# State-space layers: one PSUM tile per recurrence, B rows spread on the array's row halves, the product written one recurrence ahead

## The chip, the cores and the metric

The kernel runs on one core of a Trainium2 chip, all of it in one launch. The metric is the device time of that launch in microseconds (us), the median of several runs. The engines are named as the profile names them: PE is TensorE (matmuls; PEld is its weight load), DVE is VectorE, ACT is ScalarE, POOL is GpSimd, and SP is SyncE, which issues the DMAs.

## The reference

The input x is 4 x 64 x 128 x 128 in float32 and goes through four layers: a Mamba block with 16 states, a window-transform layer, a convolution layer with a gate, and a block of two convolutions, a Mamba with 64 states and a feed-forward part. The change is in the two Mamba parts. Cut to what matters, with 65,536 tokens and 128 inner channels:

```python
xz = u @ in_proj_w.T;  xh, z = split(xz)
xc = silu(causal_conv(xh) + conv_b)            # 4 taps, per channel
dt, B, C = split(xc @ x_proj_w.T)              # B, C: one row per state
delta = softplus(dt @ dt_proj_w.T + dt_proj_b)
A = -exp(A_log)
def step(h, t):                                # per channel d and state n
    d, b, c, xt = t
    h = h * exp(d[:, None] * A) + (d * xt)[:, None] * b[None, :]
    return h, h @ c
y = scan(step) + xc * D
y = (y * silu(z)) @ out_proj_w.T
```

Layer 0 follows it with a projection, a layer norm over the channels, SiLU and the residual; layer 3 has a layer norm ahead of it and behind it.

## The kernel before, in words

Five stages run one after the other: layer 0, layer 1, the convolutions of layers 2 and 3, layer 3's Mamba, layer 3's feed-forward part. Both Mamba stages are one class, `_Mamba`, with its own constants.

**Tiling.** The tokens are cut into 64 chunks of TC = 1024. A *recurrence* is one `tensor_tensor_scan` on 128 partitions x 1024 tokens; its partitions are NQ = 4 states x DD = 32 channels. The 128 channels take ND = 4 recurrences, which make a *group* of 4 states. A chunk has 4 groups (16 recurrences) in layer 0, 16 groups (64 recurrences) in layer 3, so there are 5120 recurrences in all. The state is carried from chunk to chunk in `state` (L584).

**What one recurrence needs.** The decay da = exp(delta A) is made by ACT (L526) from `dl`, a row copy of delta out of DRAM. The input b x delta x x is made in one of two ways, which the strings "DADA" and "DADAADAADADAADAA" choose group by group:
- *Kind A* (3072 recurrences): ACT (28 small instructions a group, L401) and POOL (one block, L405) multiply transposed channels by B into `bxT`; PE transposes it into a PSUM tile with eight instructions a recurrence (L482), and the scan reads that tile.
- *Kind D* (2048): PE spreads the four B rows of the group over the partitions once for the group, straight from xc (four 128-row matmuls, L286, called from `produced`), into one PSUM tile. DVE multiplies that tile by `du` (a row copy of delta x, L559) into a second PSUM tile, which all four recurrences use, and the scan (L577) reads this one. So mul and scan take turns.

The scan writes into a place of `ring`, which has eight places in SBUF: recurrence i uses place i mod 8. POOL multiplies the place by `cb`, the spread C rows (L582). PE then sums over the states (L427): two halves of a group, four matmuls each, into the tile y. D times xc opens y (L424). After the last group DVE makes yg = y x silu(z) (L610), and the output projection follows (L619).

**PSUM.** Three tiles of two banks, bx0 to bx2, go round a list `idle`; y takes the other two banks. The recurrences' tiles and all of the pieces below are taken from the same three.

**Order.** `run()` writes the order by hand, one recurrence after the other, and `_Pin` makes each engine keep the order of writing. In the turn of recurrence i it loads `cb` (SP), lets pieces that wait for "next" go on, writes the exps up to five recurrences ahead, the due part of `bxT` (a credit, due two recurrences before the group), for kind D the product, PE's fills up to two recurrences ahead, the scan, POOL's product, and last the sums that are due, at most one half a turn. A group's sums are due two recurrences after its last (`owed`, i + 2); yg comes one turn after the last sums (`full`, i + 1).

**Pieces.** The rest of a chunk is written as generators whose parts are put at places counted in recurrences from the chunk's first (`slots`). `front()` makes z (wz), conv (the taps), v (delta and u = delta x), C (L334, with the copy L337), B (BT, L347 and L349) and duT (L356, L358) of the next chunk. `ahead()` in layer 3 has centre and norm ahead of it, `behind()` has project and rstd (layer 0) or project, centre2 and norm2 (layer 3). A piece takes a PSUM tile, PE fills it, and at the next turn ACT reads it and gives the tile back to the end of `idle`. SP issues every load and store in that order too: `cb` (L391), `dl` and `du` (L503), the stores of delta and u (L326, L328) and of the C rows (L341).

Of the kernel before, what the change touches and what calls it, by code (L numbers as in the profile page):

```python
# [17 lines left out]
P = 128  # L18
B, C, HH, WW = 4, 64, 128, 128
HW = HH * WW  # L20
TC = 1024
# [7 lines left out]
DA = 6  # L29
_PERM = np.arange(DI).reshape(DD, ND).T.reshape(-1)  # L30
# [137 lines left out]
class _Mamba:  # L168
# [19 lines left out]
    def __init__(self, ctx, tc, K, nst, w, kinds, bufs, slots={}):  # L188
# [8 lines left out]
        self.hold, self.parts, self.shared = False, {}, None  # L197
# [17 lines left out]
        nc.vector.memset(self.wz, 0.0)  # L215
        nc.sync.dma_start(self.wz[64:], w["in_wT"][:, DI:])
        self.wbc = cp.tile([P, 2 * nst], F32, name="wbc")
        nc.sync.dma_start(self.wbc, w["xp_bcT"])
        self.wC = cp.tile([P, max(nst, DD)], F32, name="wC")
        nc.vector.memset(self.wC, 0.0)  # L220
        nc.vector.tensor_copy(self.wC[:, :nst], self.wbc[:, nst:])
        self.spread = {}
        for g in (g for g, kind in enumerate(kinds) if kind == "D"):
            s = self.spread[g] = cp.tile([P, P], F32, name=f"spread{g}")
            nc.vector.tensor_copy(
                s.rearrange("p (q e) -> p q e", q=NQ),
                self.wbc[:, NQ * g : NQ * (g + 1)].unsqueeze(2).to_broadcast([P, NQ, DD]),
            )
# [36 lines left out]
    def shift(self, b):  # L265

        for k, ws in (("conv_b", self.taps), ("z_b", [self.wz])):
            pm, col = self.pm(), self.cp.tile([P, 1], F32, name=f"{k}_shift")
            for i, wt in enumerate(ws):
                self.nc.tensor.matmul(pm[:, :1], wt, b, start=i == 0, stop=i == len(ws) - 1)  # L270
            self.nc.vector.tensor_scalar(col, pm[:, :1], getattr(self, k), None, ALU.add)
            setattr(self, k, col)
# [6 lines left out]
    def slot(self, c, name):  # L279
        return "at", c["no"] * self.ng * ND + self.slots[name]  # L280

# [13 lines left out]
    def front(self, c, S, read, before_silu=None):  # L295

        nc, K, nst = self.nc, self.K, self.nst
        xc, sz = c["xc"], c["sz"] = [self.t(k, self.bufs[k]) for k in ("xc", "sz")]
        yield self.slot(c, "z")
        pm = self.take()  # L300
        self.mm(pm, (self.wz, S[:, 2:]))
        yield "next", 0
        self.hold = True
        nc.scalar.activation(sz, pm, AF.Silu, bias=self.z_b)  # L304
        self.give(pm)
        yield self.slot(c, "conv")
        pm = self.take()
        self.mm(pm, (self.taps[0], S[:, :TC]), (self.taps[1], S[:, 2:]))
        read()
        yield "next", 0  # L310
        if before_silu:
            before_silu()
        nc.scalar.activation(xc, pm, AF.Silu, bias=self.conv_b)
        self.give(pm)
        yield self.slot(c, "v")
        pm = self.take()
        self.mm(pm, (self.wdt, xc))
        yield "next", 0
        pos, du = self.tmp("pos"), self.tmp("u")
        nc.scalar.activation(pos, pm, AF.Softplus, bias=self.dt_b)  # L320
        self.give(pm)
        nc.scalar.preload_act_table_set(SET6)
        self.hold = False
        d2 = c["d2"] = self.dram.tile([2, DI, TC], F32, name="d2", tag="d2")
        c["dl"], c["du"] = {}, {}
        nc.sync.dma_start(d2[0], pos)  # L326
        nc.gpsimd.tensor_mul(du, pos, xc)
        nc.sync.dma_start(d2[1], du)  # L328

        yield self.slot(c, "C")  # L330
        r = self.wC.shape[1]
        pm = self.take(0)
        for h in range(NH):
            nc.tensor.matmul(pm[r * h : r * (h + 1)], self.wC, xc[:, _COLS[h]], start=True, stop=True)  # L334
        yield "next", 0
        cr = self.t("cr", 1, 512)
        nc.scalar.copy(cr[: 2 * r], pm[: 2 * r])  # L337
        self.give(pm)
        c["C"] = self.dram.tile([nst, TC], F32, name="c2", tag="c2")
        for h in range(NH):  # L340
            nc.sync.dma_start(c["C"][:, _COLS[h]], cr[r * h : r * h + nst])  # L341

        yield self.slot(c, "B")
        BT = c["BT"] = self.wp.tile([P, NB, nst], F32, name="BT", tag="BT")
        pm = self.take(0)
        for k in range(NB):
            nc.tensor.matmul(pm[:, nst * k : nst * (k + 1)], xc[:, P * k : P * (k + 1)], self.wbc[:, :nst], start=True, stop=True)  # L347
        yield "next", 0
        nc.scalar.copy(BT.rearrange("p k n -> p (k n)"), pm[:, : nst * NB])  # L349
        self.give(pm)  # L350

        yield self.slot(c, "duT")
        duT = c["duT"] = self.wp.tile([P, NB, DI], F32, name="duT", tag="duT")
        pm = self.take()
        for k in range(NB):
            nc.tensor.transpose(pm[:, P * k : P * (k + 1)], du[:, P * k : P * (k + 1)], K.eye)  # L356
        yield "next", 0
        nc.scalar.copy(duT.rearrange("p k d -> p (k d)"), pm)  # L358
        self.give(pm)


    def take(self, half=None):

        if half is None:
            t = self.idle.pop(0)
            self.parts[id(t)] = [t, 1]
            return t
        if self.shared is None:
            t = self.idle.pop(0)
# [8 lines left out]
    def give(self, ap):  # L378
# [6 lines left out]
        self.idle.append(t)  # L385
# [49 lines left out]
    def run(self, chunks, ahead, behind, lead):  # L435
# [24 lines left out]
        das, tiles = {}, {}  # L460
# [15 lines left out]
        def produced(i):  # L476

            v, j = its[i]
            if v["kind"] == "A":
                bx = tiles[i] = self.idle.pop(0)  # L480
                for k in range(NB):
                    nc.tensor.transpose(  # L482
                        bx[:, P * k : P * (k + 1)], v["bxT"][:, k, :, :, j].rearrange("p q e -> p (q e)"), self.K.eye
                    )
            elif not j:
                bx = v["B"] = self.idle.pop(0)
                self.mm(bx, (self.spread[v["g"]], v["c"]["xc"]))
# [18 lines left out]
        for _ in ahead(chunks[0]):  # L506
            pass
        replicated(-1)
        pin()
        for i, (u, j) in enumerate(its):  # L510
# [9 lines left out]
            for f in [f for f in feeds if f[1][0] == "next"]:  # L520
                step(f)

            while not self.hold and nexp < min(n, i + 5) and its[nexp][1] in its[nexp][0]["c"].get("dl", ()):
# [7 lines left out]
            for v in groups[max(nmul - 1, 0) : nmul + 2]:  # L531
                if "duT" in v["c"] and v["at"] > i:
                    left += 0 if "bxT" in v else NQ * (NB - 1)
                    slope = max(slope, left / (upto[max(v["at"] - 2, i + 1)] - upto[i]))
            credit += slope * (upto[i + 1] - upto[i])
            while credit >= 0.5:
# [10 lines left out]
            credit = min(credit, 0.5)  # L547

# [4 lines left out]
            if u["kind"] == "D":  # L553
                if not j:
                    while nbx <= i:
                        produced(nbx)
                        nbx += 1
                    u["y"] = self.idle.pop(0)
                nc.vector.tensor_mul(u["y"], u["c"]["du"][j], u["B"])  # L559
                tiles[i] = u["y"]  # L560
                if j == ND - 1:
                    self.idle.append(u["B"])
            due = [f for f in feeds if f[1][0] == "at" and f[1][1] <= i] if u["kind"] == "D" and j < ND - 1 else []
            while nbx <= min(n - 1, i + 2):
                v, k = its[nbx]
                if v["kind"] == "D" and k:
                    nbx += 1
                    continue
                if nbx > i and (not self.idle or (due and len(self.idle) < 2) or (v["kind"] == "A" and (("bxT" not in v) or (todo and v is groups[nmul - 1])))):
                    break  # L570
                produced(nbx)
                nbx += 1
# [7 lines left out]
            if u["kind"] == "A" or j == ND - 1:  # L580
                self.idle.append(tiles[i])
# [4 lines left out]
            for f in due:  # L586
                step(f)
            if i == u["at"] and u["g"] == 0:
                owed.append((u["last"], u, None))
            if i == u["last"]:  # L590
                owed += [(i + 2, u, h) for h in range(NH)]
            while owed and not full and (owed[0][0] <= i or i + 1 == n):
                _, v, h = owed.pop(0)
                self._sums(v, h)
                if v["g"] == self.ng - 1 and h == NH - 1:
                    full = i + 1, v["c"]
                if i + 1 < n:
                    break
            replicated(i)
# [26 lines left out]
def layer0(ctx, tc, K, w, x, x1):  # L626
    nc = tc.nc
    slots = {"z": -16, "conv": -15, "v": -14, "C": -8, "B": -7, "duT": -6, "project": 24, "rstd": 25}
    m = _Mamba(ctx, tc, K, 16, w, "DADA", {"xc": 2, "sz": 3, "tmp": 4}, slots)
# [53 lines left out]
    def behind(c, yg):  # L683
        c["res"] = m.t("res", 2, 512)
        for h, src in enumerate(_halves(x[c["at"][0]], c["at"][1])):
            nc.sync.dma_start(c["res"][64 * h : 64 * (h + 1)], src)
# [14 lines left out]
        m.give(pm)  # L701
        nc.gpsimd.tensor_mul(o, pc, o)

# [572 lines left out]
def layer3_mamba(ctx, tc, K, w, t3, x3, s3, n3):  # L1276

    nc = tc.nc
    slots = {"centre": -44, "norm": -43, "z": -32, "conv": -31, "v": -30, "C": -24, "B": -23, "duT": -22}
    slots |= {"project": 72, "centre2": 73, "norm2": 74}  # L1280
    m = _Mamba(ctx, tc, K, 64, w, "DADAADAADADAADAA", {"xc": 2, "sz": 2, "tmp": 4}, slots)
# [23 lines left out]
    def ahead(c):  # L1305
# [23 lines left out]
        m.give(pm)  # L1329
        nc.gpsimd.tensor_mul(S[:, 2:], xs, sq)  # L1330
# [5 lines left out]
    def behind(c, yg):  # L1336
        b, t0 = c["at"]
        tr, xr = m.t("tr", 1, 512), m.t("xr", 1, 512)
# [14 lines left out]
        xs, o = m.t("ncr", 1, 512), m.t("o", 1, 512)  # L1353
# [8 lines left out]
        m.give(pm)  # L1362
        nc.gpsimd.tensor_mul(o, xs, o)
# [287 lines left out]
```

## Time and profile before

| | |
|---|---|
| device time, median of three runs | 18174.38 us (18161.99 to 18198.42) |
| profiled execution: its own time, its span | 18180.54 us, 18178.8 us |
| granted TensorE clock, mean | 0.892 |
| busy share PE, PEld, DVE, ACT, POOL | 78%, 39%, 86%, 79%, 76% |
| layer 0: yg products (L610), first 426.2 to tenth 880.6 us | 50.45 us a chunk |
| layer 3: yg products, 5827.0 to 17220.7 us for 64 | 180.85 us a chunk |

The profile records one execution. The span is the time from its first to its last instruction. Each group of instructions is a line of the kernel with an engine, an operation, the tile written and the tiles read; a wait is the idle time of an engine ahead of an instruction, with the instruction that released it. The share of busy time is an average over five stages with different limits, so the stages are looked at separately, in windows of the trace. The clock is what the throttle granted PE, as a share of full speed.

### The profile page before, as it was taken

How to read it: one execution, taken by the hardware profiler on the slowest of the kernel's cores; microseconds unless marked ns; L12 is line 12 of the kernel's file. 1: busy time of each engine (PE TensorE's matmuls, PEld its weight loads, DVE VectorE, ACT ScalarE, POOL GpSimd, SP SyncE). 2: the span in 40 equal slices, each digit the busy share in tenths (PEclk: the TensorE clock that was granted, in tenths of full speed). 3: DMA queues.
4: the chain of work that ended last, by engine and by line, in shares of the span. 5: the costliest groups of instructions: out<-in, count | busy, mean ns of one | idle time of the engine just before them, and what ended most of it. 6: DMA issues, size and time to landing. Idle time of an engine off the chain costs nothing. (4 is left out here: it accounts for less than half of the span.)

```text
span 18178.8 us, 232945 instructions
## 1 busy us (share of the span) xinstructions
PE 14201.9 (78%) x77626; PEld 7167.2 (39%) x77626; DVE 15626.1 (86%) x8611; ACT 14325.0 (79%) x29853; POOL 13839.1 (76%) x7966
## 2 busy tenths in 40 slices
PE   7788788798997777777777777777777777777799
PEld 3333333387344333333333333333333333333333
DVE  8999999522116999999999999999999999999987
ACT  8888889212336999999999999999999999999733
POOL 7888889300005999999999999999999999999800
PEclk9999999789998888888888888898888888888899
DMA  6666666211212333232333333323333333333222
GB/s 162 168 167 170 168 168 172 66 44 59 70 40 81 90 82 92 81 91 82 90 83 90 84 88 84 88 84 89 84 88 84 88 84 89 84 89 83 74 55 55
DMA packets 669499, 1722.52 MB, mean 95 GB/s; under 512 B 196784, under 2 KB 231936, under 8 KB 660864
## 3 DMA queue, kind: packets, MB, share of 16 engines
q1 hardware_dynamic: 668288, 1707.62, 34.6%
q8 instruction: 608, 9.96, 0.2%
q14 instruction: 603, 4.94, 0.1%
HBM read 1434.27 MB, written 272.63 MB: 94 GB/s over the span
## 5 line engine op out<-in xcount | busy, mean ns | idle before, releaser
L582 POOL TENSOR_TENSOR ring<-ring,cb 128x1024 f32<-128x1024 f32 x5120 | 12048.3, 2375 | 1119.3 <-DVE ring L577 1064.3
L577 DVE TENSOR_TENSOR_SCAN ring<-da,state,bx 128x1024 f32<-128x1024 f32 x4848 | 11070.8, 2332 | 343.4 <-PE bx L482 83.6
L401 ACT ACTIVATE bxT<-duT,BT 128x128 f32<-128x128 f32 x21504 | 6770.9, 388 | 110.2 <-PE bx L482 110.2
L526 ACT ACTIVATE da<-dl,A 128x1024 f32<-128x1024 f32 x5120 | 5809.7, 1139 | 501.1 <-DVE ring L577 483.6
L482 PE MATMUL bx<-cst,bxT 128*128 128x128 f32 x24576 | 4101.7, 320 | 1947.7 <-DVE bx L559 861.1
L482 PEld LDWEIGHTS bx<-cst,bxT 128*128 128x128 f32 x24576 | 3490.8, 212 | 3626.3 <-DVE ring L577 1474.3
L427 PE MATMUL y<-ring,cst 128*32 128x512 f32 x20480 | 3548.2, 671 | 336.7 <-POOL ring L582 336.6
L559 DVE TENSOR_TENSOR bx<-du,bx 128x1024 f32<-128x1024 f32 x2048 | 2503.3, 1222 | 131.1 <-ACT da L526 47.8
L427 PEld LDWEIGHTS y<-ring,cst 128*32 128x32 f32 x20480 | 517.5, 113 | 1885.3 <-POOL ring L582 833.2
L1143 PE MATMUL cv<-img,cw 64*64 64x512 f32 x9216 | 1010.1, 595 | 73.1 <-DMA img<-d_x 45.6
L286 PE MATMUL bx<-xc,spread 128*128 128x512 f32 x2048 | 1019.5, 620 | 0.2
L1301 POOL MEMSET X<- 64x1 f32 x4 | 0.4, 102 | 1123.4 <-DMA cw<-in_l_conv_wT 1123.4
L405 POOL TENSOR_TENSOR bxT<-duT,BT 128x512 f32<-128x512 f32 x768 | 803.8, 1047 | 6.4 <-ACT duT L358 6.4
L347 PE MATMUL bx<-wbc,xc 128*128 128x16 f32 (+1 forms) x2048 | 391.3, 360 | 449.1 <-ACT cr L337 333.0
L1068 POOL TENSOR_TENSOR xs<-xs,cl 128x1024 f32<-128x1024 f32 x32 | 75.9, 2371 | 861.8 <-DVE cl L1067 861.8
L286 PE MATMUL bx<-S,cw 128*128 128x512 f32 x1024 | 536.0, 671 | 248.2 <-ACT sz L304 248.2
L1143 PEld LDWEIGHTS cv<-img,cw 64*64 64x64 f32 x9216 | 490.9, 134 | 590.5 <-issue 479.4
L1438 POOL MEMSET h<- 128x18 f32 x64 | 8.3, 132 | 875.1 <-PE pd L1526 443.0
L1452 ACT ACTIVATE h<-ph,ff_fc_b 128x384 f32<-128x384 f32 (+1 forms) x384 | 200.7, 577 | 593.2 <-PE ph L1447 575.4
L286 PEld LDWEIGHTS bx<-xc,spread 128*128 128x128 f32 x2048 | 349.9, 191 | 760.4 <-issue 476.4
L1526 PE MATMUL pd<-h,diag 64*64 64x512 f32 x4608 | 631.6, 602 | 0.7 <-issue 0.7
L577 DVE TENSOR_TENSOR_SCAN ring<-da,bx 128x1024 f32<-128x1024 f32 x272 | 604.7, 2272 | 31.0 <-PE bx L482 10.2
(311 smaller groups left out, 10931.8 us busy)
## 6 DMA issues: line engine op xcount, KB each, us to landing
cb<-c SPq DMA_DIRECT2D x5120, 128.0 KB, 2.9
dl<-d SPq DMA_DIRECT2D x2048, 128.0 KB, 3.4
du<-d SPq DMA_DIRECT2D x2048, 128.0 KB, 3.3
d<-pos SPq DMA_DIRECT2D x128, 512.0 KB, 3.0
d<-u SPq DMA_DIRECT2D x128, 512.0 KB, 3.0
X<-d_t SPq DMA_DIRECT2D x124, 256.0 KB, 4.1
S<-in_x SPq DMA_DIRECT2D x120, 256.5 KB, 3.9
res<-in_x SPq DMA_DIRECT2D x128, 128.0 KB, 3.2
```

Source lines behind the costliest of these rows:

```text
L286: self.nc.tensor.matmul(out[: l.shape[1], k : k + 512], l, r[:, k : k + 512], start=i == 0, stop=i == len(pairs) - 1)
L347: nc.tensor.matmul(pm[:, nst * k : nst * (k + 1)], xc[:, P * k : P * (k + 1)], self.wbc[:, :nst], start=True, stop=True)
L401: nc.scalar.activation(t[:, k, q].rearrange("p e j -> p (e j)"), c["duT"][:, k, :], AF.Copy, scale=c["BT"][:, k, n : n + 1])
L405: nc.gpsimd.tensor_mul(t[:, k].rearrange("p q e j -> p q (e j)"), c["duT"][:, k].unsqueeze(1).to_broadcast(shape), c["BT"][:, k, NQ * g : ...
L427: nc.tensor.matmul(c["y"][DD * j : DD * (j + 1), _COLS[h]], K.sel, hc[:, _COLS[h]], start=False, stop=u["g"] == self.ng - 1,)
L482: nc.tensor.transpose(bx[:, P * k : P * (k + 1)], v["bxT"][:, k, :, :, j].rearrange("p q e -> p (q e)"), self.K.eye)
L526: nc.scalar.activation(das[nexp], v["c"]["dl"][k], AF.Exp, scale=self.A[:, k, v["g"] : v["g"] + 1])
L559: nc.vector.tensor_mul(u["y"], u["c"]["du"][j], u["B"])
L577: nc.vector.tensor_tensor_scan(hs, das.pop(i), tiles[i], 0.0 if u["c"].get("reset") else st, ALU.mult, ALU.add)
L582: nc.gpsimd.tensor_mul(hc, hs, u["cb"])
L1143: nc.tensor.matmul(p[i][half[h]], W[half[i], k, :], src[half[i], at : at + 4, dx : dx + WW], start=k == 0, stop=k == 8,)
L1526: nc.tensor.matmul(pd[i][half[h]], diag[half[i], k, :], h0[half[i], r : r + 4, dx : dx + WW], start=k == 0, stop=k == 8,)
```

## The change

It is confined to `_Mamba` and the two stages that use it.

- Each D recurrence gets a PSUM tile of its own, like an A recurrence. B and C rows are projected together, once a chunk, by `wboth`, and copied by ACT into an SBUF tile `bc`, on both halves of the partitions. From there two matmuls per recurrence spread the four rows of the group: half h of the tokens uses the array's rows 64h and up (`rows`, the new `spread`, which is a selection out of the identity).
- DVE multiplies in place (`times`), and the product of recurrence i+1 is written ahead of the scan of i, wherever its tile was filled in an earlier turn.
- z is projected on the two row halves too (`wz` on both).
- PE's fills for the turn come in two parts, one ahead of the scan and one after it and after the sums. Tiles that pieces give back go to a list `late` and become idle with the scan's tile.
- Pieces get other places: conv ahead of z; B before duT before C in layer 3; the C rows at -11 instead of -24; the pieces behind one to three recurrences later. ACT's reads of pieces come after the exps, in layer 3 after up to three `bxT` parts. The product u and the norm products on POOL come one turn later, and the residual's load of layer 0 later still, with one buffer. In layer 3, xc has one buffer instead of two, and four small tiles come from the shared `tmp`.
- Sums are due three recurrences after a group's last instead of two, yg two turns after the last sums instead of one, and `bxT` is due four recurrences before its group instead of two.

The diff, cut to its core:

```diff
+BEHIND = 2
+LATER = 3
+EXPS = 5
+DUE = 4
...
+        for h in range(NH):
+            for k in range(2):
+                a = DD * k if self.small else 64 * (h ^ k)
+                nc.vector.tensor_copy(self.wboth[:, h, a : a + nst], self.wbc[:, nst * k : nst * (k + 1)])
...
+    def rows(self, bc, h, k):
+        a = 64 * h + DD * k if self.small else 64 * (h ^ k)
+        return bc[a : a + self.nst, :512] if self.small else bc[a : a + self.nst, _COLS[h]]
...
+        def both(pm):
+            for h in range(NH):
+                out = pm[64 * h : 64 * (h + 1), :512] if self.small else pm[:, _COLS[h]]
+                nc.tensor.matmul(out, self.wboth[:, h], xc[:, _COLS[h]], start=True, stop=True)
...
+    def free(self):
+        if not self.idle:
+            self.idle, self.late = self.late, []
+        return self.idle.pop()
...
-        self.idle.append(t)
+        self.late.append(t)
...
+            else:
+                for h in range(NH):
+                    r = slice(64 * h, 64 * h + self.nst)
+                    nc.tensor.matmul(bx[:, _COLS[h]], self.spread[v["g"]][r], self.rows(v["c"]["B"], h, 0), start=True, stop=True)
+
+        def times(k):
+            v, j = its[k]
+            if v["kind"] == "D" and k not in done:
+                done.add(k)
+                nc.vector.tensor_mul(tiles[k], v["c"]["du"][j], tiles[k])
+
+        def fill(i, upto):
+            nonlocal nbx
+            while nbx < min(n, upto) and self.idle:
+                v = its[nbx][0]
+                if nbx > i and v["kind"] == "A" and ("bxT" not in v or (todo and v is groups[nmul - 1])):
+                    break
+                if nbx > i and v["kind"] == "D" and "B" not in v["c"]:
+                    break
+                produced(nbx, i)
+                nbx += 1
...
-            if u["kind"] == "D":
-                if not j:
-                    while nbx <= i:
-                        produced(nbx)
-                        nbx += 1
-                    u["y"] = self.idle.pop(0)
-                nc.vector.tensor_mul(u["y"], u["c"]["du"][j], u["B"])
-                tiles[i] = u["y"]
...
+            fill(i, max(i + 1, min(nbx + 1, i + 3)))
+            times(i)
+            if i + 1 < n and filled.get(i + 1, i) < i:
+                times(i + 1)
             slot = i % (2 * ND)
...
-            if u["kind"] == "A" or j == ND - 1:
-                self.idle.append(tiles[i])
+            fresh = len(self.idle)
+            self.idle += [tiles[i]] + self.late
+            self.late = []
...
-                owed += [(i + 2, u, h) for h in range(NH)]
+                owed += [(i + LATER, u, h) for h in range(NH)]
...
-                    full = i + 1, v["c"]
+                    full = i + BEHIND, v["c"]
...
+            free, self.idle = self.idle[fresh:], self.idle[:fresh]
+            fill(i, i + 3)
+            self.idle += free
+            for f in [f for f in feeds if f[1][0] == "at" and f[1][1] <= i]:
+                step(f)
...
-    slots = {"z": -16, "conv": -15, "v": -14, "C": -8, "B": -7, "duT": -6, "project": 24, "rstd": 25}
+    slots = {"conv": -16, "z": -14, "v": -13, "C": -8, "B": -6, "duT": -5, "project": 24, "rstd": 26}
...
-    slots = {"centre": -44, "norm": -43, "z": -32, "conv": -31, "v": -30, "C": -24, "B": -23, "duT": -22}
-    slots |= {"project": 72, "centre2": 73, "norm2": 74}
+    slots = {"centre": -43, "norm": -41, "conv": -32, "z": -30, "v": -28, "B": -23, "duT": -21, "C": -11}
+    slots |= {"project": 73, "centre2": 75, "norm2": 77}
```

## The prediction

> **What bounds the kernel now.** I read the page's groups first. VectorE (DVE) is busy 86% of the span, and most of that is one scan per recurrence (L577) and, for 2048 of the 5120 recurrences, one product ahead of it (L559). The columns are busy us, mean ns, idle us before, and what ended the idle time.
>
> ```profile
> L577 DVE TENSOR_TENSOR_SCAN ring<-da,state,bx 128x1024 f32<-128x1024 f32 x4848 | 11070.8, 2332 | 343.4 <-PE bx L482 83.6
> L559 DVE TENSOR_TENSOR bx<-du,bx 128x1024 f32<-128x1024 f32 x2048 | 2503.3, 1222 | 131.1 <-ACT da L526 47.8
> ```
>
> Then I read two windows, layer 0 in steady state and the layer-3 state-space stage (columns: window, length, busy us of PE, PEld, DVE, ACT, POOL, granted clock, DMA share, GB/s). VectorE is the fullest engine in both, at 97% in the second; only there does work saved on it shorten the span.
>
> ```profile
> 400.00:3000.00 2600.00, 2084.04 (x10398) 970.22 (x10399) 2442.87 (x1289) 2323.60 (x4433) 2311.16 (x1289) 0.93 0.65 168
> 6200.00:17200.00 11000.00, 8197.02 (x41282) 4126.62 (x41283) 10679.69 (x5412) 10071.52 (x22002) 10267.47 (x5841) 0.88 0.31 86
> ```
>
> The periods come from the 64 yg products. Layer 3: (17220.7-5827.0)/63 = 180.85 us a chunk. Layer 0: ten from 426.2 to 880.6, nine intervals, 50.45 us. In them POOL is busy 168.8 and 44.8 us, ACT 165.6 and 45.1, PE 134.8 and 40.4.
>
> Then VectorE's timeline, across one D group and into A recurrences (start, length, instruction):
>
> ```profile
> 10034.36 1.21 DVE L559 TENSOR_TENSOR bx<-du,bx 128x1024 f32<-128x1024 f32 x1
> 10035.71 2.35 DVE L577 TENSOR_TENSOR_SCAN ring<-da,state,bx 128x1024 f32<-128x1024 f32 x1
> 10038.09 1.23 DVE L559 TENSOR_TENSOR bx<-du,bx 128x1024 f32<-128x1024 f32 x1
> ...
> 10168.82 1.20 DVE L610 TENSOR_TENSOR yg<-y,sz 128x1024 f32<-128x1024 f32 x1
> 10169.94 1.22 DVE L559 TENSOR_TENSOR bx<-du,bx 128x1024 f32<-128x1024 f32 x1
> ```
>
> In the D group mul to scan is 10035.71-10034.36 = 1.35 us (others 1.36), scan to the next mul 2.38: each is held by the one before, since the product waits for the shared tile and the scan for the product. A mul that nothing holds follows L610 after 1.12. A scans in a row start 2.24 apart although each lasts 2.35. So a D group takes 10046.93-10034.36+2.24 = 14.81 us, and VectorE's floor is 40x2.24+6x14.81+1.12 = 179.58 us in layer 3 (1.27 of 180.85 is stall) and 8x2.24+2x14.81+1.12 = 48.66 in layer 0 (1.79 of 50.45).
>
> Last, the waits. In layer 3 little holds VectorE (82.7 us in 11,000), so its stall is small; in layer 0 it waits for TensorE's sums, and ScalarE waits for TensorE's pieces:
>
> ```profile
> DVE ring L577 <- PE bx L482: 82.7, 62, 2.4
> ```
> ```profile
> ACT xc L313 <- PE bx L286: 132.2, 52, 4.7
> ACT BT L349 <- PE bx L286: 96.8, 51, 3.3
> DVE yg L610 <- PE y L427: 92.4, 29, 4.8
> ```
>
> [...] eight transposes take 1.23 or 1.98 us and eight sums matmuls 1.07 or 1.94. [...] four 64-row matmuls of 384 columns (L1447) take 0.92 us, four 128-row ones of 512 (L286) 1.98.
>
> **The change, part by part.**
>
> 1. *Product one recurrence ahead.* All but 192 of the 2048 muls now stand ahead of the previous scan, in a tile of their own. A pair costs 1.12+2.24 = 3.36 us, a group 13.44: 1.37 less. The 192, where a piece holds a tile, remain next to their scan (1.36, 0.24 more each), one per chunk in layer 3, two in layer 0. Layer 3: 6x1.37-0.24 = 7.98, floor 171.60. Layer 0: 2x1.37-2x0.24 = 2.26, floor 46.40. Over 64 chunks of each: 655 us. I take this in full.
>
> 2. *B rows spread per recurrence.* A D group had one spread of four matmuls (1.98 us); it now has four pairs of 64-row matmuls. Its price between 0.5 (side by side, full clock) and 2.0 (one after the other, half); I take 1.1, from L1447. PE grows by 4x1.1-2.0 = 2.4 per group, some 11 with smaller edits: 146 of 171.6, not the bound. A spread starts at a scan's end and its mul comes 3.36 us later, so 1.1+0.2 is covered by the mul and scan between; at 2.0 it still is. Without that cover (the 192) it costs up to 1.5. One copy of B and C on ACT (1.0 for 0.56 us) is 0.45 a chunk in layer 3, hidden by ACT's 15 us of room.
>
> 3. *Sums three recurrences late, not two.* The four-matmul halves (L427) stand on PE behind a fill that itself waits for a scan. The ring has eight places, so a group's first scan waits for the sums of the group two before. With two, the fill's scan lay three recurrences back; now it lies two back. So the chain scan end, fill, sums, next scan is set beside one scan of 2.24 us:
>
> ```profile
> 10051.57 1.23 PE L482 MATMUL bx<-cst,bxT 128*128 128x128 f32 x8 [0.63 <-DVE ring L577]
> 10052.73 1.07 PE L427 MATMUL y<-ring,cst 128*32 128x512 f32 x8
> ...
> 10018.84 1.98 PE L482 MATMUL bx<-cst,bxT 128*128 128x128 f32 x8 [0.26 <-DVE ring L577]
> 10020.75 1.94 PE L427 MATMUL y<-ring,cst 128*32 128x512 f32 x8
> ```
>
> Full clock: 0.16 (scan end to fill)+1.16+1.06-2.24 = 0.14. Half: 0.16+1.91+1.93-2.24 = 1.76. A head with a mul just ahead of its scan has cover, so I count those without: nine a chunk, eight plain and one behind the BT piece (L347) too. The clock is 1.00 or 0.50 in short windows, so 0.88 means 24% half; PE gets fuller, so I take 15% (bounds 5 to 53). A plain head costs 0.14+0.15x1.62 = 0.38, eight 3.1. The ninth waits behind BT's 16 matmuls (3.0 us); between 0.9 and 3.4, I take 2.0. In layer 0 one head stands behind BT and rstd: 1.3 to 3.25, I take 1.8. Lower bound for all: nothing, if PE runs ahead.
>
> 4. *Pieces moved.* Two old stalls go: 1.27 behind the duT piece in layer 3, and 1.79 in layer 0, where yg waited for sums behind conv (5.40 us of PE at 1028.20). They are not counted again, since I start from floors. What is late next is the conv piece, now ahead of z: 0.7 in layer 3, 0.4 in layer 0 (nothing to 1.5). The C row loads get about 11 recurrences, 27 us, against 2.9 of landing. The product u (POOL) and its store, res, and the norm products come a recurrence later, and their readers at least seven; SP issues as many DMAs, POOL and SP have the same queue behind them otherwise. Zero, covered by those recurrences; if this cover failed, some 3 us a chunk.
>
> **Sum.** Layer 3: 171.60+3.1+2.0+0.7 = 177.4, 3.45 less, 221 us. Layer 0: 46.40+1.8+0.4 = 48.6, 1.85 less, 118 us. Together 339 off the profiled execution's 18180.5 (span 18178.8): 17,842. The median of the runs, 18174.4, is 6 lower, so I say 17,840. Own range 17,600 to 18,060: the stalls of 3 and 4 halved give some 17,600; those of the slow clock at 30% with upper ends for BT and conv some 18,060.
>
> **Rivals.**
> - *The full gain stays* (0.19). Sums are ahead of need and only the conv piece and a BT rest show: layer 3 172.5, layer 0 47: 64x(8.35+3.45) = 755 off, about 17,430. For it: PE has 25 us of room a chunk. Against: VectorE already runs within 1.27 of its floor, so any new PE delay shows at once.
> - *Slower: sums behind a waiting fill at the group heads* (0.18). Nine heads break even at 3.45+5.8 = 9.3 us a chunk, 1.03 each, which is a half-clock share near 53%. If the new order leaves PE waiting on scans more often and the share is 70%, layer 3 is near 184 to 186 and layer 0 50: about 18,490. For it: stretches like 10016 to 10022 are at half clock just where PE waits for each scan. Against: 0.88 on average.
> - *ScalarE bounds layer 0.* Its 45.1 and the 265 us in 51.5 chunks that it waits for PE (5.15) make 50.2, so layer 0 gains nothing: 17,960, inside my own range. POOL's 168.8 lies under 171.6 and 177 and does not decide.
> - *Gains and stalls cancel* (0.06): 18,140 to 18,216.
> - *It doesn't do what it says*: excluded, since the order of instructions has 1856 muls ahead.
>
> **How the numbers follow.** Likeliest case 0.57, with ScalarE's; full gain 0.19; cancel 0.06; slower 0.18. A measurement here tells about 0.2%, 36 us, from no change. So faster 0.76, same 0.06, slower 0.18. The range, 17,430 to 18,330, takes in the full gain's centre and the lower part of the slower case. It leaves out about 0.08 below and 0.11 above.
>
> **What would show it.** Right: muls start 1.12 before a scan and 2.24 after one, a D group takes 13.44 us, yg comes every 177 and 48.6 us, and VectorE's new waits are for the sums at group heads, some 3 to 5 us a chunk. Wrong: D pairs at 3.7 (step 1), muls waiting for spreads (2), no wait for sums or one over 1 us a head (3), yg still waiting for sums (4), or a clock far from 0.9.

## The result and the profile after

The changed kernel is slower: 18803.43 us, median of four runs (18789.44 to 18810.32), against 18168.19 before (now of four runs); the ratio is 1.0346, with a 95% interval of 1.0328 to 1.0363. The forecast was faster, 17,840, with a range that ended at 18,330.

The profiled execution took 18807.81 us, 627 more than that of before. By the first and last scan of each stage in the two traces, 207 us of this lie in layer 0 and 416 in layer 3's Mamba; the other stages are within 6. From the scan starts of the 60 middle chunks the periods are 53.8 us in layer 0 (50.4 before) and 187.6 in layer 3 (181.0).

The same lines of the page's groups as before (busy us, mean ns, idle us ahead, what ended it). The scan's idle time has gone from 343 to 1100 us, and TensorE's sums end it:

```profile
L628 DVE TENSOR_TENSOR_SCAN ring<-da,state,bx 128x1024 f32<-128x1024 f32 x4848 | 11136.1, 2332 | 1100.1 <-PE y L467 1000.0
L529 PE MATMUL bx<-bc,spread 64*128 64x512 f32 (+1 forms) x8192 | 2650.3, 730 | 1597.9 <-DVE ring L628 1561.6
L535 DVE TENSOR_TENSOR bx<-du,bx 128x1024 f32<-128x1024 f32 x2048 | 2477.7, 1210 | 309.5 <-PE bx L529 145.7
```

The second line holds the other half of the story: the short spreads (L529) have 1598 us of idle TensorE ahead of them. The two windows of before, taken again (length, busy us of PE, PEld, DVE, ACT, POOL, granted clock, DMA share, GB/s). VectorE is busy less and TensorE more; the clock fell from 0.93 to 0.83 in layer 0 and from 0.88 to 0.86 in layer 3:

```profile
400.00:3000.00 2600.00, 2252.34 (x10923) 1002.03 (x10922) 2260.20 (x1210) 2181.71 (x4148) 2164.08 (x1209) 0.83 0.61 158
6200.00:17200.00 11000.00, 8543.82 (x44106) 4000.79 (x44105) 10133.95 (x5221) 9751.79 (x21234) 9934.02 (x5639) 0.86 0.31 83
```

VectorE's timeline over the end of a D group and its head (the first scan of the next group, of kind A), start and length:

```profile
9998.21 2.33 DVE L628 TENSOR_TENSOR_SCAN ring<-da,state,bx 128x1024 f32<-128x1024 f32 x1
10000.46 1.20 DVE L535 TENSOR_TENSOR bx<-du,bx 128x1024 f32<-128x1024 f32 x1
10001.58 2.33 DVE L628 TENSOR_TENSOR_SCAN ring<-da,state,bx 128x1024 f32<-128x1024 f32 x1
...
10004.94 4.57 DVE L628 TENSOR_TENSOR_SCAN ring<-da,state,bx 128x1024 f32<-128x1024 f32 x2
10011.46 2.35 DVE L628 TENSOR_TENSOR_SCAN ring<-da,state,bx 128x1024 f32<-128x1024 f32 x1 [1.95 <-PE y L467]
```

Scan to mul is 2.25 us and mul to scan 1.12, as step 1 of the prediction had it. Then the head at 10011.46 waits 1.95 us. TensorE over the same time:

```profile
9997.23 1.13 PE L529 MATMUL bx<-bc,spread 64*128 64x512 f32 x4 [1.24 <-DVE ring L628]
10000.59 1.13 PE L529 MATMUL bx<-bc,spread 64*128 64x512 f32 x4 [2.24 <-DVE ring L628]
10003.97 1.98 PE L673 MATMUL bx<-tx,cst 128*64 128x512 f32 x4 [2.24 <-DVE ring L628]
10005.72 1.93 PE L674 MATMUL bx<-yg,woT 128*64 128x512 f32 x4
10007.58 1.61 PE L467 MATMUL y<-ring,cst 128*32 128x512 f32 x8
10009.12 1.23 PE L523 MATMUL bx<-cst,bxT 128*128 128x128 f32 x8
10010.27 1.07 PE L467 MATMUL y<-ring,cst 128*32 128x512 f32 x8
```

A spread takes 1.13 us and TensorE then sits idle for 2.24 us until the next scan gives a tile back. After two such stretches the project piece runs at half rate (L673, 1.98 us for four matmuls, at a granted clock of 0.50), and behind it stand one half of the sums, a fill and the other half, for which the scan at 10011.46 waits. 30 us later the drop from 1.00 to 0.50 can be seen: the same spread takes 1.13, then 2.08, and the centre piece behind it 3.78 where it took 1.98 before:

```profile
10030.90 1.13 PE L529 MATMUL bx<-bc,spread 64*128 64x512 f32 x4 [1.24 <-DVE ring L628]
10034.27 2.08 PE L529 MATMUL bx<-bc,spread 64*128 64x512 f32 x4 [2.24 <-DVE ring L628]
10037.64 3.78 PE L301 MATMUL bx<-X,cst 128*128 128x512 f32 x4 [1.29 <-DVE ring L628]
```

### The profile page after: what moved, and what is told of

It is laid out like the page before. It is cut to its first block, busy times and chain, and to the rows that moved or that the text cites. A ratio compares the mean times of both kernels' runs of the same rounds, so it can differ in the third digit from the quotient of the medians.

```text
span 18806.0 us, 244842 instructions
## 1 busy us (share of the span) xinstructions
PE 15270.9 (81%) x83770; PEld 7295.5 (39%) x83770; DVE 15397.7 (82%) x8623; ACT 14362.4 (76%) x29853; POOL 13859.8 (74%) x7966
## 4 chain that ended last, share of the span: by engine, by line
PE 25%; DVE 21%; ACT 10%; issue 8%; DMA 2%; POOL 1%; SPq 1%; DVEq 0%; POOLq 0%; ACTq 0%
DVE ring L628 15%; PE bx L523 6%; DVE bx L535 6%; PE y L467 6%; ACT da L584 4%; ACT bxT L441 4%; PE bx L301 4%; PE pd L1586 3%; PE bx L357 1%; PE bx L352 1%; DMA cb<-c 1%; POOL ring L634 1%; PE ph L1507 1%; PE bx L673 1%; PE po L1551 1%
## 5 line engine op out<-in xcount | busy, mean ns | idle before, releaser
L584 ACT ACTIVATE da<-dl,A 128x1024 f32<-128x1024 f32 x5120 | 5734.2, 1138 | 353.4 <-DVE ring L628 333.7
L523 PE MATMUL bx<-cst,bxT 128*128 128x128 f32 x24576 | 3774.3, 303 | 719.6 <-DVE ring L628 656.2
L523 PEld LDWEIGHTS bx<-cst,bxT 128*128 128x128 f32 x24576 | 3288.5, 210 | 2664.3 <-DVE ring L628 1696.7
L529 PE MATMUL bx<-bc,spread 64*128 64x512 f32 (+1 forms) x8192 | 2650.3, 730 | 1597.9 <-DVE ring L628 1561.6
L467 PE MATMUL y<-ring,cst 128*32 128x512 f32 x20480 | 3117.6, 683 | 7.8 <-POOL ring L634 7.8
L535 DVE TENSOR_TENSOR bx<-du,bx 128x1024 f32<-128x1024 f32 x2048 | 2477.7, 1210 | 309.5 <-PE bx L529 145.7
L529 PEld LDWEIGHTS bx<-bc,spread 64*128 64x128 f32 (+1 forms) x8192 | 696.7, 206 | 3189.0 <-DVE ring L628 2850.0
L467 PEld LDWEIGHTS y<-ring,cst 128*32 128x32 f32 x20480 | 429.7, 115 | 1630.6 <-issue 1228.7
L301 PE MATMUL bx<-S,cw 128*128 128x512 f32 x1024 | 702.7, 851 | 298.2 <-DVE ring L628 285.2
L1532 DVE SCALAR_TENSOR_TENSOR g<-h,dww,g 128x2048 f32<-128x2048 f32 x256 | 601.9, 2351 | 11.0
```

The lines of the kernel that those rows point to most:

```text
L301: self.nc.tensor.matmul(out[: l.shape[1], k : k + 512], l, r[:, k : k + 512], start=i == 0, stop=i == len(pairs) - 1)
L467: nc.tensor.matmul(c["y"][DD * j : DD * (j + 1), _COLS[h]], K.sel, hc[:, _COLS[h]], start=False, stop=u["g"] == self.ng - 1,)
L523: nc.tensor.transpose(bx[:, P * m : P * (m + 1)], v["bxT"][:, m, :, :, j].rearrange("p q e -> p (q e)"), self.K.eye)
L529: nc.tensor.matmul(bx[:, _COLS[h]], self.spread[v["g"]][r], self.rows(v["c"]["B"], h, 0), start=True, stop=True)
L535: nc.vector.tensor_mul(tiles[k], v["c"]["du"][j], tiles[k])
L584: nc.scalar.activation(das[nexp], v["c"]["dl"][k], AF.Exp, scale=self.A[:, k, v["g"] : v["g"] + 1])
```

## The experiments

Four theories were set against each other: **A**, the sums come too late for the ring, because they are due one recurrence later and stand behind fills and pieces; **B**, TensorE is too slow altogether; **C**, the sums hold the fills while they wait for POOL; **D**, the clock is the cause. A time without an interval is that of one execution; executions of one kernel differ by 0.2% here (18160 to 18198 us before the change), and the differences between such times that a conclusion rests on are larger.

**later2**: the sums due as before the change.

```diff
-LATER = 3
+LATER = 2
```

> The changed kernel with the sums of a group due two recurrences after its last, as before the change, and nothing else altered. Theory A (the loss is the ring: a group's first scan waits for the sums of the group two before, and these now come one recurrence later, behind a fill or a piece that itself waits for a scan): each half gets one scan of 2.24 us more, so the waits of scans for L467 fall from some 13 us a layer-3 chunk to under 4 and from 4.8 to under 2.6 in layer 0; the periods go from 187.6 to about 177 and from 53.8 to about 51, and the time to 17,850 to 18,100 us. Theory B (TensorE is too slow in all: half clock and more matmuls, the waiting scan only shows it): the waits move to the muls or to other heads, and the time stays above 18,600 us. Theory C (the sums now wait for POOL's products and hold the fills behind them): waits of scans for L523 instead, time near 18,400.

Measured 18685.32, clock 0.882. That is 118 us under the changed kernel, outside what theory A gave and inside theory B's. The scans' wait for L467 is gone, but most of it has come back elsewhere. The waits in the layer-3 window (us, times, longest):

```profile
DVE bx L535 <- PE bx L529: 601.9, 270, 5.6
PEld y L467 <- POOL ring L634: 522.5, 347, 2.7
DVE ring L628 <- PE bx L523: 137.2, 159, 2.5
```

Sums written earlier wait on TensorE for POOL's last product, and the spreads and fills behind them are late instead. This is theory C, on another line than I named (the muls' more than the scans').

**before_later3**: the kernel before, with one constant changed.

```diff
-                owed += [(i + 2, u, h) for h in range(NH)]
+                owed += [(i + 3, u, h) for h in range(NH)]
```

> The kernel before, with its sums due three recurrences after the group's last instead of two. Theory A in its plain form (the later sums alone make the wait): scans wait for L427 at the group heads, at least 5 us a layer-3 chunk, so over 18,450 us. Theory A with the tiles (the delay needs the new tile scheme as well, where TensorE can't run ahead in D groups because each spread waits for a scan): the kernel before hardly notices, within 60 us of its time.

Measured 18928.31, 764 us over before, with the clock at 0.869 (0.892 before). The plain form of A holds for the old tiles: later sums alone cost more than the whole change does (764 against 635 us). In layer 3:

```profile
DVE ring L577 <- PE y L427: 494.4, 408, 2.7
```

That is 494.4/11000x192 = 8.6 us a chunk. So the due time of the sums suits one tile scheme and harms the other, and can't be judged by itself.

**no_ahead**: the changed kernel without the product ahead.

```diff
-            if i + 1 < n and filled.get(i + 1, i) < i:
-                times(i + 1)
```

> The changed kernel with each product directly ahead of its own scan, all else kept. VectorE's floor rises by some 8.2 us a layer-3 chunk and 2.3 a layer-0 chunk. Theory A (sums late by a fixed chain on TensorE): the longer D groups give the chain time, the waits for L467 at heads behind D groups fall by about as much, and the time stays within 150 us of the changed kernel's 18,803. Rival (the waits are independent of VectorE's pace): the floor's rise adds in full, about 18,803+64x10.5 = 19,470 us.

Measured 18436.08, *faster* than with the product ahead by 367 us, outside both expectations. The clock is 0.880. The product ahead had made each D pair shorter, and VectorE only waited longer at the heads: its waits for L467 in the layer-3 window are 308.6 us here and 707.6 in the changed kernel.

**full_rows**: the D spreads on the whole array; z stays on row halves.

```diff
-                    nc.tensor.matmul(bx[:, _COLS[h]], self.spread[v["g"]][r], self.rows(v["c"]["B"], h, 0), start=True, stop=True)
+                    nc.tensor.matmul(bx[:, _COLS[h]], self.spread[v["g"]][:, h], bc if self.small else bc[:, _COLS[h]], start=True, stop=True)
```

> The changed kernel with the D spreads on all 128 rows of the array: the selection has zeros in the other half's rows, so two matmuls of 128 rows stand in place of two on row halves, one after the other. Theory D (half the array at work lets the clock fall, and the slow clock makes the waits): the granted clock returns to 0.88 or more in layer 3 and over 0.90 in layer 0, against 0.86 and 0.83, and the time falls below 18,700. Theory A: the clock follows from TensorE's idle stretches, not from the rows, so it rises little; each spread costs up to 1 us more on TensorE and the time is the same or rises, to 18,800 to 19,200.

Measured 18154.87, 649 us under the changed kernel. A spread that takes *longer* (1.98 for 1.13 us) gives back all of the loss (before took 18164.41 beside it). The clock is at 1.00 and 0.99, and the scans' wait for the sums in layer 3 fell from 707.6 to 191.8 us. The windows, the wait (changed kernel first), and TensorE in a D group:

```profile
400.00:3000.00 2600.00, 2334.95 (x11513) 1072.35 (x11506) 2365.66 (x1273) 2294.96 (x4379) 2281.35 (x1272) 1.00 0.64 166
6200.00:17200.00 11000.00, 9060.26 (x45971) 4386.08 (x45970) 10567.45 (x5445) 10148.48 (x22106) 10360.75 (x5877) 0.99 0.32 86
```
```profile
DVE ring L628 <- PE y L467: 707.6, 468, 4.0
...
DVE ring L629 <- PE y L468: 191.8, 490, 1.6
```
```profile
10018.24 1.99 PE L530 MATMUL bx<-bc,spread 128*128 128x512 f32 x4
10021.40 1.98 PE L530 MATMUL bx<-bc,spread 128*128 128x512 f32 x4 [1.17 <-DVE ring L629]
10024.77 1.09 PE L674 MATMUL bx<-tx,cst 128*64 128x512 f32 x4 [1.39 <-DVE ring L629]
```

The D pair of VectorE is 3.37 us. A spread of 1.98 leaves 1.39 of it idle, one of 1.13 leaves 2.24; here the same project piece takes 1.09. Theory D stands, B falls: TensorE has more to do and the kernel is faster. Whether it is the rows or the time was still open.

**halves_twice**: row halves, each matmul issued twice.

```diff
+                    for _ in range(2):
+                        nc.tensor.matmul(bx[:, _COLS[h]], self.spread[v["g"]][r], self.rows(v["c"]["B"], h, 0), start=True, stop=True)
```

> The changed kernel with every spread matmul on a row half issued twice in a row (the second overwrites the first with the same values), so TensorE is busy about as long per spread as with full rows (some 2 us against 1.13), but with half of the rows. Theory D1 (rows: matmuls on 64 rows do not hold the clock up): the clock stays at 0.86 or lower in layer 3 and about 0.83 in layer 0, and with the longer spreads the time rises, to 18,900 or more. Theory D2 (busy time: what held the clock with full rows is only that TensorE idles less): the clock rises to 0.95 or more, and the time falls to about 18,150 to 18,300.

Measured 18315.73, 16 us above the range of D2. With nothing but useless work added, the kernel gains 488 us, so TensorE's busy time counts, as D2 has it:

```profile
400.00:3000.00 2600.00, 2417.82 (x12632) 1100.38 (x12634) 2286.25 (x1225) 2210.33 (x4213) 2195.15 (x1225) 0.94 0.62 160
6200.00:17200.00 11000.00, 9098.47 (x51750) 4444.40 (x51746) 10548.03 (x5432) 10151.12 (x22093) 10341.99 (x5865) 0.98 0.32 87
```
```profile
10021.18 1.99 PE L530 MATMUL bx<-bc,spread 64*128 64x512 f32 x8
10024.32 1.99 PE L530 MATMUL bx<-bc,spread 64*128 64x512 f32 x8 [1.14 <-DVE ring L629]
```

In layer 3 it is as good as full rows (clock 0.98, 180.3 us a chunk against 179.6). But this says nothing of the rows there: the matmuls of the two halves run side by side (in the changed kernel's trace one starts at 9997.227 and the other at 9997.233, and each takes 0.69 us), 64 rows each. In layer 0 a spread uses only 16 rows in each half, and there the clock is 0.94 and not 1.00, although TensorE is busier (93% against 90%). The spreads of layer 0, halves_twice first:

```profile
L530 PE MATMUL bx<-bc,spread 16*128 16x512 f32 x3134 | 794.1, 623 | 24.4 <-DVE ring L629 21.8
...
L530 PE MATMUL bx<-bc,spread 128*128 128x512 f32 x1627 | 796.7, 612 | 74.1 <-DVE ring L629 71.6
```

They are busy equally long, on 16 rows and on 128. I read this as D1 in part, the rows counting beside the busy time. That was not shown: the number of matmuls differs too, and no run tests the rows alone.

**full_no_ahead**: full rows, each product directly ahead of its own scan (the edit of no_ahead).

> Spreads on full rows, and each product directly ahead of its own scan. With the full clock the waits at the group heads are small, so if step 1 is right, its gain must show here: 8.2 us a layer-3 chunk and up to 2.3 a layer-0 chunk are lost again, less the waits that longer D groups absorb (at most 2 to 4 us): 18,155 plus 64x(5 to 9), so 18,450 to 18,750 us. If the product ahead is worth nothing even at the full clock, it is within 100 us of 18,155.

Measured 18428.71, 274 us over full_rows (just below what I expected); layer 3's period is 184.1 against 179.6, layer 0's 50.9 against 51.1. At the full clock the product ahead is worth 4.5 us a layer-3 chunk and nothing in layer 0. That is not half of step 1's 8.0 lost: this edit undoes only a part of step 1, since each recurrence keeps a tile of its own. Scan to mul is not held (2.27 us), and mul to scan is 1.31:

```profile
10013.27 2.35 DVE L627 TENSOR_TENSOR_SCAN ring<-da,state,bx 128x1024 f32<-128x1024 f32 x1
10015.54 1.21 DVE L536 TENSOR_TENSOR bx<-du,bx 128x1024 f32<-128x1024 f32 x1
10016.85 2.35 DVE L627 TENSOR_TENSOR_SCAN ring<-da,state,bx 128x1024 f32<-128x1024 f32 x1
```

A pair is 3.58 us, against 3.37 with the product ahead. Over six groups of four that is 5.0 us a chunk, of which 4.5 show in the period.

**full_first** and **full_later2**: full rows, and the sums earlier, in two ways. In full_first the block that writes the sums stands ahead of the turn's first fill:

```diff
+            while owed and not full and owed[0][0] <= i and i + 1 < n:
+                _, v, h = owed.pop(0)
+                self._sums(v, h)
+                if v["g"] == self.ng - 1 and h == NH - 1:
+                    full = i + BEHIND, v["c"]
+                break
             fill(i, max(i + 1, min(nbx + 1, i + 3)))
...
-            while owed and not full and (owed[0][0] <= i or i + 1 == n):
+            while owed and not full and i + 1 == n:
```

> Spreads on full rows, and in each turn the due half of the sums ahead of the fill that waits for the scan before, no longer behind it. The chain at a group head loses one fill: theory A predicts that the waits of scans for the sums, 4.4 us a layer-3 chunk and 2.8 a layer-0 chunk with full rows, go below 1 each, and the time falls to 17,750 to 17,900 us. Rival (the sums then hold the fills, waiting for POOL's products): waits for L523's or the spread's line grow by as much, and the time stays at 18,100 or more.

> Spreads on full rows, and the sums due two recurrences after a group's last. Theory A: waits of scans for the sums vanish; but as in the run on row halves the sums now stand on TensorE waiting for POOL's last product, ahead of the fills: 13.7 us of stalls a layer-3 chunk there, of which I expect a third to a half at the full clock. So 17,900 to 18,250 us, not better than the order with the sums first in the turn.

Measured 18667.47 and 18570.61, 513 and 416 us worse than full_rows, at clocks of 0.969 and 0.977. Both expectations were too low, and full_first's rival was right. In full_first (layer 3) the sums wait for POOL, and the muls for the spreads behind them:

```profile
DVE bx L536 <- PE bx L530: 760.1, 371, 4.4
PEld y L468 <- POOL ring L642: 480.1, 405, 2.7
```

At the full clock, both ways of writing the sums earlier cost more than they save with the new tiles.

**mixed** and **mixed2**: full rows, except for the first recurrence of each D group (mixed), or for the first and the last (mixed2).

```diff
+                    if not j:                      # mixed2: if j in (0, ND - 1)
+                        r = slice(64 * h, 64 * h + self.nst)
+                        nc.tensor.matmul(bx[:, _COLS[h]], self.spread[v["g"]][r, h], self.rows(bc, h, 0), start=True, stop=True)
+                    else:
                         nc.tensor.matmul(bx[:, _COLS[h]], self.spread[v["g"]][:, h], bc if self.small else bc[:, _COLS[h]], start=True, stop=True)
```

> Spreads on full rows, except that of each D group's first recurrence, which stays on row halves. With full rows the muls that wait for a spread are those of group heads: some 3.2 us a layer-3 chunk and 0.9 in layer 0; there the shorter spread (1.13 for 1.98 us) takes up to 0.85 off each. If TensorE's idle time sets the clock, one spread in four shorter leaves it at 0.95 or more: 18,155 less 64x(1.5 to 2.7), so 17,980 to 18,080 us. If a little more idle time is enough to lose the clock, it falls under 0.93 and the time rises over 18,250.

> Row halves for the first and the last recurrence of each D group, full rows for the two between. It asks how much shorter the spreads may be before the clock goes. Clock theory: it lies between the full rows' 0.975 and the changed kernel's 0.863, at 0.91 to 0.95, and the time at 18,150 to 18,400. If it stays at 0.95 or more, the time is like that of one spread in four on halves, 17,950 to 18,080.

Measured 17974.96 (ratio to before 0.9887, 0.9872 to 0.9902) and 18556.48 (1.0209, 1.0193 to 1.0224). mixed came as expected (5 us under its range) and is 1.1% faster than the kernel before: 177.5 us in layer 3 and 50.5 in layer 0. mixed2, with one more short spread in four, loses 582 us against it; its clock is in the range of the clock theory, its time above it. The layer-3 windows, mixed first:

```profile
6200.00:17200.00 11000.00, 8956.39 (x46780) 4259.43 (x46784) 10663.70 (x5511) 10149.58 (x22099) 10312.08 (x5882) 0.98 0.32 87
```
```profile
6200.00:17200.00 11000.00, 8958.81 (x44468) 4194.20 (x44472) 10211.06 (x5259) 9814.25 (x21393) 10007.74 (x5679) 0.90 0.31 84
```
```profile
10000.40 1.98 PE L524 MATMUL bx<-cst,bxT 128*128 128x128 f32 x8 [2.24 <-DVE ring L633]
```

TensorE's total busy time is the same within 3 us of 11,000, yet the clock is 0.98 and 0.90. (It is not the same work: 44,468 matmuls took as long at 0.90 as 46,780 at 0.98.) What differs is how the idle time is cut up. mixed2 has idle stretches of 2.24 us again (third line: the fill after one takes 1.98, not 1.23). The trace also has the granted clock itself. In the traces of before and of the changed kernel it is 1.00 or 0.50, for 3.41 us or a multiple of that at a time. Counted in the layer-3 window, with how many of the falls came behind 3.41 us in which TensorE was busy under half of the time:

| kernel | PE idle | idle stretches over 2.0 us | clock | falls to half clock | of these, behind 3.41 us busy under half |
|---|---|---|---|---|---|
| before | 25% | 293 | 0.88 | 461 | 452 |
| after | 22% | 422 | 0.86 | 413 | 412 |
| mixed2 | 19% | 296 | 0.90 | 377 | 363 |
| mixed | 19% | 2 | 0.98 | 114 | 102 |
| halves_twice | 17% | 0 | 0.98 | 100 | 50 |
| full_no_ahead | 18% | 0 (284 between 1.60 and 1.63) | 0.98 | 146 | 93 |
| full_rows | 18% | 0 | 0.99 | 86 | 44 |

So the number of idle stretches over 2.0 us does not account for the falls by itself: mixed has two of them and falls 114 times. In the changed kernel's window none exceeds 2.24 us, and the clock is 0.86 all the same. There TensorE was busy under half of the 3.41 us ahead of 412 of the 413 falls. Each of the 412 intervals of 3.41 us at full clock that were busy under half was followed by half clock, and of the 1872 others one was; in the trace of before 63 of 516 such intervals were not. A turn of 1.13 us busy and 2.24 idle is busy for a third, one of 1.98 and 1.39 for 59%. With full rows only 44 of 86 falls came so and with doubled spreads 50 of 100; the others follow intervals busy 50 to 71%, which stays open. In layer 0 the count is another one: in the changed kernel 55 of the 97 falls of the window 400 to 3000 us follow intervals busy 53 to 85%, with doubled spreads all 64 follow intervals busy 66 to 84%, and with full rows there is no fall.

**mixed_l0** and **mixed_l3**: mixed, with pieces moved.

```diff
-    slots = {..., "C": -8, "B": -6, "duT": -5, "project": 24, "rstd": 26}
+    slots = {..., "C": -8, "B": -5, "duT": -4, "project": 24, "rstd": 27}
...
-    slots = {"centre": -43, "norm": -41, "conv": -32, "z": -30, "v": -28, ...}
+    slots = {"centre": -44, "norm": -42, "conv": -33, "z": -31, "v": -29, ...}
```

> As the version with each group's first spread on row halves, and in layer 0 the pieces B, duT and rstd one recurrence later, so that BT's and rstd's matmuls come after the sums that the group head 12 waits for and not between their halves. Theory A (pieces ahead of sums on TensorE make the layer-0 head wait, 2.26 us with full rows): that wait goes under 0.7, layer 0 falls by 1.0 to 1.6 us a chunk, and the time is 60 to 100 us under that version's. Rival (the later duT delays bxT and so the next A group, or the C and project pieces take the tile instead): no gain, or a loss, with waits for L524's line.

> As the version with each group's first spread on row halves, and in layer 3 the pieces centre, norm, conv, z and v one recurrence earlier. With full rows the heads 28 and 36 and the mul of 40 wait 1.14, 0.72 and 2.15 us, each behind a tile that norm, z or v holds until ACT has read it. Theory A: an earlier piece gives its tile back one scan earlier, and two thirds of these waits go: 2 to 3 us a chunk, 130 to 190 us under that version's time. Rival (any place in a D group holds one of three tiles for as long, and the wait only moves to another head): within 60 us of it, either way.

Measured 18042.81 (0.9925, 0.9908 to 0.9941) and 18097.45 (0.9954, 0.9939 to 0.9969): 68 and 122 us over mixed. In layer 0 the head's wait fell as expected (2.26 to 0.57 us a chunk), but later ones took its place: 1.56 for a late fill two recurrences on and 0.81 at a mul, mostly for its du load. In layer 3 the waits at 28 and 36 went, and others of 1.3 to 1.9 came at 24, 34 and 38. The rivals had the mechanism right: with three tiles a moved piece moves the wait. mixed_l3 lost twice what its rival allowed.

## Why the prediction was wrong

- **What bounds the kernel**: right. VectorE's chain stayed the place where time is won and lost.
- **Step 1** (product ahead): its floor was right. The period less all excess over the unheld spacings is 171.4 us in layer 3 (I had 171.60) and 45.9 in layer 0 (46.40). At the full clock the part of it that full_no_ahead undoes is felt almost in full (4.5 of 5.0 us). What failed is that it would be so at any clock: in the changed kernel the product ahead cost 367 us (no_ahead).
- **Step 2** (spread on row halves): the duration was right, 1.13 us for 1.1; TensorE's busy time in layer 3, 8543.82/11000x187.6 = 145.7 us for 146, agrees in part by luck, since more of it ran at half rate than I took. That a cheap spread can do no harm was the error that decided: I asked only whether it comes in time, and not what TensorE does in the rest of the 3.36 us pair. The rest is up to 2.24 us of idling, in every D group.
- **Step 3** (sums later) is the term that was mis-sized, by way of its clock. "PE gets fuller, so I take 15%" is the step that failed: TensorE did get fuller (78% busy in the layer-3 window for 75%), and half rate rose to 28% and 34% of the time (clocks of 0.86 and 0.83). And I spread it evenly over the heads, where it falls in the D groups and just behind them: by the trace, 48 to 72% of the sums matmuls ahead of the heads 4, 12, 24, 44 and 56 ran at half clock, and at most 1% of those ahead of the other five. The excess of five of the six heads behind a D group (4, 12, 24, 44, 56) is 1.5 to 2.7 us, about my half-clock price of 1.76 and more where a piece stands ahead (36 has 0.7, after a wait of 1.0 at a mul); three of those behind an A group (16, 48, 60) stand at 0.21 to 0.26, near my full-clock price of 0.14. The ten heads of A groups together are 13.3 us a chunk against my 5.1 for nine, and in layer 0 the head at 12 is 4.7 against 1.8. At the full clock (full_rows) the ten are 4.5, below my sum.
- **Step 4** (pieces): the conv piece was not the late one. In layer 3, 1.0 us was lost at the mul of 35 for its spread and 1.2 at the mul of 40, which the profile puts down to ScalarE (L584); in layer 0, 1.3 at a mul for its spread and 0.7 for ScalarE's sz. 0.7 and 0.4 were forecast. I had all but excluded muls that wait for spreads.
- **The sum**: the misses, 187.6-177.4 and 53.8-48.6 over 64 chunks of each, make 986 us. 17,842 and 986 are 18,828, against the profiled 18,808.
- **The rivals**: the slower one named the mechanism that won, sums behind a fill at heads at half rate, with 18,490 and a chance of 0.18. Its break-even share (53%; from its own figures (1.03-0.14)/1.62 is 55%) was the same error as in step 3: 28% were enough, since they fell on the heads. "ScalarE bounds layer 0" fell: in layer 0 too the scans wait for sums.

full_rows took 18,155, not 17,840. So some 650 us of the loss go with the short spreads and their clock, and some 315 are a gain that isn't there even at the full clock, because other waits take its place: excess over the unheld spacings of 8.2 us in layer 3 (I had 5.8) and 5.2 in layer 0 (I had 2.2).

## What to carry to other kernels

- Work on an engine with a varying clock has two prices: its duration, and the idle stretch that it leaves behind. When a change shortens an instruction in a loop paced by another engine, subtract it from the loop's period and ask what a longer stretch does. Here stretches of 2.24 us went with a kernel 3.5% slower than before, and stretches of 1.39 us with one as fast as before.
- Don't spread a mean clock evenly over the waits. Look at the instructions just behind the idle stretches: here the slow sums stood there, 48 to 72% of them at half clock ahead of five heads.
- A lag such as "sums three recurrences late" is right only together with the tiles and the order around it: it cost the old scheme 764 us, and taking it out of the new one gained 118 us with the short spreads and cost 416 at the full clock.

## What the runs showed of the hardware

In layer 3 TensorE's clock did not go with its mean share of busy time: at 19% idle in both, mixed2 with 296 idle stretches of over 2.0 us had a clock of 0.90, and mixed with two had 0.98. In the changed kernel 412 of 413 falls to half clock came behind 3.41 us in which TensorE was busy under half of the time; with full rows 44 of 86 did. In layer 0, where a short spread uses 16 rows in each half, the clock of the kernel with doubled spreads also fell behind intervals busy 66 to 84%; whether the rows at work stand behind this was not shown. Issuing the same short matmuls twice raised the mean clock from 0.863 to 0.962 and took 488 us off the time. At the full clock a recurrence's spread took 1.13 us on row halves and 1.98 on all rows; the matmuls of the two halves, 0.69 us each, start 0.01 us apart, so they ran side by side.
